# A graph network's prologue: degrees read one group later, x in fourteen buffers, its later groups loaded from ScalarE

## The chip, the cores and the metric

The kernel runs on one core of a Trainium2 chip. The metric is the device time of one execution in microseconds (us). One execution of the kernel before was also taken by the hardware profiler; its page and its trace are what the prediction reads.

## The reference

A graph of 12,500 nodes with 256 features and 200,000 edges, sorted by destination, goes through a three-layer graph convolution on the normalised features, with a residual, and then through a mixture of experts whose gates come from attention over a second edge list. What matters here is the start of the first part:

```python
deg_inv_sqrt = jnp.where(deg > 0, jax.lax.rsqrt(jnp.maximum(deg, 1.0)), 0.0)   # deg: edges into a node, and its own loop
norm = deg_inv_sqrt[src] * deg_inv_sqrt[dst]
h = x @ W
msg = h[src] * norm[:, None]
out = jax.ops.segment_sum(msg, dst, num_segments=n_nodes)   # + b; gelu after layers 1 and 2
...
x = x + _L0_gnn_ref(_layernorm(x, axis=-1), edge_index, ...)
```

So before the first layer can gather a row, every row of x must be normalised by its own mean and deviation and scaled by the square root of its node's degree, and the degrees have to be counted from the edge list.

## The kernel before

The nodes are cut into 98 tiles of 128 rows. The tiles go in 14 groups of seven (`groups`, `ROW_GROUP = 7`); the last tile is partly empty. Line numbers are those of the profile.

**The search.** `load_keys` reads sources and destinations, packs each edge into one key word, and `put_keys` writes the keys to DRAM (`keys_a`). If the edges had not been sorted, a branch (L611) would sort them; here it is jumped over. `starts` then finds each tile's first edge: it reads the first key of each of 128 rows (`a_first`, L426, issued from ScalarE), compares, gathers one whole row per tile (`a_row`, L438, an indirect transfer from GpSimd), and counts the keys below the tile's bound (L443). `mine` (L452) gathers each tile's keys, TensorE transposes them (L734), and VectorE makes from them the source numbers `a_src` and, as two small numbers `hi_p` and `lo_p`, each edge's place in its tile.

**x and the norms.** `xn` is one buffer for all 98 tiles. `load_x` fills it on SP's queue (L525, L528): `groups[:5]` before the branch in the program's text, the others after it; the scheduler has put two of those ahead of the branch as well. `norm(first, n)` takes mean and variance of `n` groups on VectorE (L589, L590) and the square root on ScalarE (L592). The calls are laid out by hand as filling between the steps of the search: groups 0 and 1, 2 and 3, 4 and 5, then 6 and 7 beside the degrees' way through DRAM, and 8 to 13 in the scaling loop.

**The count.** A loop over seven groups of 16 tiles (`TG16`, a grouping of its own) builds 24 one-hot pieces on VectorE (L782, L786; two buffers of each kind), multiplies them in 18 products on TensorE (L792) into a PSUM tile (`deg_ps`, two buffers), and reads the tile back on VectorE with a mask and a sum (L795, L797). `counts` is written to DRAM (L801) from SP and ScalarE, read back across partitions as `deg_t` (L804), and transposed; its inverse square root is `dis`.

**The scaling loop** (L1267 to L1288). For each group: three small VectorE instructions, then seven row tiles scaled and shifted, two on GpSimd, one on VectorE, four on ScalarE, and one write of the group to `tables[0]` on SP's queue (L1285). After all 14 groups, SP writes the same rows again, as `bases[0]`, each node's own share of the sum (L1288).

**The first layer.** `xn`'s room is then given back and used for the layers' tiles. A loop over overflow edges (`beyond`, no turns with these inputs) stands before the layer; its exit waits for what is under way. `cols_s` (L889) is GpSimd's first instruction after it, and then come the gathers from `tables[0]` (L1474), one per 128 edges, which go on through all three layers.

The order inside the stretches under `tc.manual_schedule()` is the order of the text; each engine runs its own instructions in order. SP and ScalarE both issue transfers; a transfer's issue waits until the one eight before it, over both, has landed.

Of the kernel before, what the change touches and what calls it, by code (L numbers as in the profile page):

```python
# [8 lines left out]
F32 = mybir.dt.float32  # L9
# [3 lines left out]
OP = mybir.AluOpType  # L13
AX = mybir.AxisListType
# [5 lines left out]
P = 128  # L20
D = 256
# [9 lines left out]
ROW_GROUP = 7  # L31
# [7 lines left out]
TG16 = 16  # L39
# [27 lines left out]
def gnn_ffn_kernel(  # L67
# [24 lines left out]
    nc = tc.nc  # L92
    N = x.shape[0]
    NT = (N + P - 1) // P
# [28 lines left out]
    groups = [(t, min(t + ROW_GROUP, NT)) for t in range(0, NT, ROW_GROUP)]  # L123
# [11 lines left out]
    CAP = caps[0] + (SPILL + P - 1) // P  # L135
# [381 lines left out]
        yield  # L517
        nc.vector.reciprocal(rstd, rstd)

    def load_x(t, g0, g1):  # L520
        if g1 * P > N:
            nc.vector.memset(t[:, : g1 - g0], 0.0)
        whole = min(g1, N // P)
        if whole > g0:
            nc.sync.dma_start(t[:, : whole - g0],  # L525
                              x[g0 * P : whole * P].rearrange("(t p) d -> p t d", p=P))
        if whole < g1:
            nc.sync.dma_start(t[: N - whole * P, whole - g0], x[whole * P : N])  # L528

    x2_d = dram.tile([NT * P, D], F32, name="x2_d")  # L530
    ht_d = dram.tile([M, ROW], F32, name="ht_d")
# [37 lines left out]
    bases = [dram.tile([NT, P, D], F32, name=f"base{i}") for i in range(3)]  # L569

    xn_cm = tc.tile_pool(name="xn", bufs=1)
    xn = xn_cm.__enter__().tile([P, NT, D], F32, name="xn")


    pre = ExitStack()
# [5 lines left out]
    rs = prep.tile([P, NT], F32, name="rs")  # L581
    sh = prep.tile([P, NT], F32, name="sh")
    SOONER = 5

    def norm(first, n):
        for g0, g1 in groups[first : first + n]:
            for t in range(g0, g1):
                six = prep.tile([P, 6], F32, name="six0", bufs=2)
                nc.vector.bn_stats(six, xn[:, t, :])  # L589
                nc.vector.bn_aggr(mv[:, t, :], six)  # L590
            nc.vector.tensor_scalar(rs[:, g0:g1], mv[:, g0:g1, 1], LN_EPS, None, op0=OP.add)
            nc.scalar.activation(rs[:, g0:g1], rs[:, g0:g1], AF.Sqrt)  # L592

    keys_cm = tc.tile_pool(name="keysA", bufs=1)
    with keys_cm as pool, tc.manual_schedule():
        key, n_falls = load_keys(pool, "a_", src, dst, EA, shifted=True)
        for g0, g1 in groups[:SOONER]:
            load_x(xn[:, g0:g1], g0, g1)
        none = pool.tile([P, tail_a], F32, name="none")
        nc.vector.memset(none, NO_EDGE)  # L600
        nc.scalar.dma_start(keys_a[EA:].rearrange("(p c) -> p c", p=P), none)
        put_keys(keys_a, key, EA)
        ps = lps.tile([P, P], F32, name="list_ps")
        for j in range(2):
            nc.tensor.matmul(ps[:1, :1], n_falls[:, j : j + 1], ones[:, 0:1], start=(j == 0),
                             stop=(j == 1))
        falls_i = prep.tile([1, 1], I32, name="falls_i")
        nc.vector.tensor_copy(falls_i, ps[:1, :1])
    unsorted = nc.values_load(falls_i[0:1, 0:1], min_val=0, max_val=EA,
                              skip_runtime_bounds_check_because="a count of edges")  # L610
    with tc.If(unsorted > 0):  # L611
        with tc.tile_pool(name="sortA", bufs=1) as pool, tc.tile_pool(
            name="sortA_ps", bufs=2, space=PSUM
# [20 lines left out]
    lpool = lists.enter_context(tc.tile_pool(name="lists", bufs=1))  # L634
    finding = starts(lpool, lps, "a_", keys_a, LA)
    next(finding)
    for g0, g1 in groups[SOONER:]:
        load_x(xn[:, g0:g1], g0, g1)
    norm(0, 2)
    next(finding)  # L640
    norm(2, 2)
    try:
        next(finding)
    except StopIteration as done:
# [1 line left out]
    nc.vector.tensor_copy(start_i, start_a)  # L646
    mine = lpool.tile([P, CAP * P + 1], F32, name="mine")
    read_keys(mine, keys_a, start_i[:, 0:1])
    norm(4, 2)


    spill = prep.tile([P, 12], F32, name="spill")
# [2 lines left out]
    ps = lps.tile([P, P], F32, name="list_ps")  # L655
# [12 lines left out]
    ps = lps.tile([P, P], F32, name="list_ps")  # L668
# [5 lines left out]
    ps = lps.tile([P, P], F32, name="list_ps")  # L674
# [13 lines left out]
    ps = lps.tile([P, P], F32, name="list_ps")  # L688
# [41 lines left out]
    for k0 in range(0, CAP, KG):  # L730
        n = min(KG, CAP - k0)
        ps = lps.tile([P, KG, NTP], F32, name="turn_ps")
# [18 lines left out]
    LO = 16  # L751
# [12 lines left out]
    with tc.tile_pool(name="deg", bufs=1) as pool, tc.tile_pool(  # L764
        name="deg_ps", bufs=2, space=PSUM
    ) as dps, tc.manual_schedule():
        same_i = pool.tile([P, 1], I32, name="same_i")
        nc.vector.tensor_scalar(same_i, pcol_i, TG16 - 1, None, op0=OP.bitwise_and)
        same_c = pool.tile([P, 1], F32, name="same_c")
        nc.vector.tensor_copy(same_c, same_i)  # L770
        same = pool.tile([P, TG16], F32, name="same")
        nc.vector.tensor_scalar(same, cols[:, :TG16], same_c, None, op0=OP.is_equal)
        counts = pool.tile([P, NTP // TG16, LO], F32, name="counts")
        NG = NTP // TG16
        step = 1
        for g0 in range(0, NG, step):
            n = min(step, NG - g0)
            w = slice(g0 * TG16, (g0 + n) * TG16)
            A = pool.tile([P, CAP, step, HI, TG16], BF16, name="hi_one", bufs=2)
            B = pool.tile([P, LO, CAP, step * TG16], BF16, name="lo_one", bufs=2)  # L780
            for v in range(HI):
                nc.vector.tensor_scalar(  # L782
                    A[:, :, :n, v, :], hi_p[:, :, w].rearrange("p k (g t) -> p k g t", t=TG16),
                    float(v), None, op0=OP.is_equal)
            for v in range(LO):
                nc.vector.tensor_scalar(B[:, v, :, : n * TG16], lo_p[:, :, w], float(v), None,  # L786
                                        op0=OP.is_equal)
            for g in range(n):
                s = slice(g * TG16, (g + 1) * TG16)
                ps = dps.tile([P, LO, TG16], F32, name="deg_ps")  # L790
                for k in range(CAP):
                    nc.tensor.matmul(ps, A[:, k, g].rearrange("p a t -> p (a t)"), B[:, :, k, s], start=(k == 0),  # L792
                                     stop=(k == CAP - 1))
                diag = pool.tile([P, LO, TG16], F32, name="diag", bufs=2)
                nc.vector.tensor_tensor(diag, ps, same[:, None, :].to_broadcast([P, LO, TG16]),  # L795
                                        op=OP.mult)
                nc.vector.tensor_reduce(counts[:, g0 + g, :], diag, axis=AX.X, op=OP.add)  # L797
        deg_v = deg_d.rearrange("(g t a b) -> a t g b", t=TG16, a=HI, b=LO)
        for a in range(HI):
            eng = nc.sync if a % 2 else nc.scalar  # L800
            eng.dma_start(deg_v[a], counts[a * TG16 : (a + 1) * TG16])  # L801
        norm(6, 2)
        deg_t = pool.tile([NTP, P], F32, name="deg_t")
        nc.scalar.dma_start(deg_t, deg_d.rearrange("(t p) -> t p", p=P))  # L804
        ps = lps.tile([P, P], F32, name="list_ps")
        nc.tensor.transpose(ps[:, :NTP], deg_t, ident[:NTP, :NTP])

        nc.vector.tensor_scalar(dis, ps[:, :NTP], 1.0, None, op0=OP.add)
# [456 lines left out]


    with tc.manual_schedule():  # L1267
        known = 8
        for i, (g0, g1) in enumerate(groups):
            if i + 1 >= known and i + 1 < len(groups):  # L1270
                norm(i + 1, 1)
            w = slice(g0, g1)
            nc.vector.reciprocal(rs[:, w], rs[:, w])
            nc.vector.tensor_tensor(rs[:, w], rs[:, w], dis[:, w], op=OP.mult)
            nc.vector.scalar_tensor_tensor(sh[:, w], mv[:, w, 0], -1.0, rs[:, w], op0=OP.mult,
                                           op1=OP.mult)
            for t in range(g0, g1):
                row, scale, shift = xn[:, t, :], rs[:, t : t + 1], sh[:, t : t + 1]
                if t % ROW_GROUP in (1, 4):
                    nc.gpsimd.tensor_scalar(row, row, scale, shift, op0=OP.mult, op1=OP.add)  # L1280
                elif t % ROW_GROUP == 6:
                    nc.vector.tensor_scalar(row, row, scale, shift, op0=OP.mult, op1=OP.add)
                else:
                    nc.scalar.activation(row, row, AF.Identity, bias=shift, scale=scale)
            nc.sync.dma_start(tables[0][g0 * P : g1 * P].rearrange("(t p) d -> p t d", p=P),  # L1285
                              xn[:, g0:g1, :])
        for g0, g1 in groups:
            nc.sync.dma_start(bases[0][g0:g1].rearrange("t p d -> p t d"), xn[:, g0:g1, :])  # L1288
    pre.close()
    xn_cm.__exit__(None, None, None)  # L1290

# [1 line left out]
    with tc.tile_pool(name="gwork", bufs=3) as work, tc.tile_pool(  # L1293
        name="gmsg", bufs=8
    ) as msg, tc.tile_pool(name="ghot", bufs=8) as hot, tc.tile_pool(name="later", bufs=1) as later, tc.tile_pool(
        name="sps", bufs=1, space=PSUM
    ) as sps, tc.tile_pool(name="gps_m", bufs=2, space=PSUM) as ps_m, tc.tile_pool(
        name="gps_d", bufs=3, space=PSUM
# [7 lines left out]
        for i, a in enumerate((att_src, att_dst)):  # L1306
# [4 lines left out]
                                    op=OP.mult)  # L1311
            nc.vector.tensor_reduce(wg[:, :, HE + i * HEADS : HE + (i + 1) * HEADS],
                                    wa.rearrange("p k (h e) -> p k h e", e=EXPERTS),
                                    axis=AX.X, op=OP.add)
# [114 lines left out]
        for layer in range(3):  # L1429
# [22 lines left out]
            with tc.manual_schedule():  # L1452
# [14 lines left out]
                for t in range(NT):  # L1467
                    pm = ps_m.tile([P, D + QUAD], F32, name="pm")
                    cap = caps2[t] if layer else caps[t]
                    for k in range(0, cap, QUAD):  # L1470
                        n = min(QUAD, cap - k)
# [9 lines left out]
                        else:  # L1481
# [3 lines left out]
                                         stop=False)  # L1485
                        for i in range(n):
                            nc.tensor.matmul(pm[:, :D], oh[:, i], m[:, i], start=False,  # L1487
                                             stop=False)
# [3 lines left out]
                        if k:  # L1492
                            i = k // QUAD - 1
# [16 lines left out]
                    for i in range(used):  # L1510
                        nc.tensor.matmul(pm[:, :D], oh[:, i], shared[:, i], start=False,  # L1511
                                         stop=(i == used - 1))
# [600 lines left out]
```

## Time and profile before

| What | Value |
|---|---|
| three timed runs, us | 7752.15, 7755.71, 7757.81 (median 7755.71) |
| the profiled execution, us | 7752.2, its span on the core 7750.4 |
| GpSimd busy | 5592.8 us (72%) |
| TensorE busy | 5482.8 us (71%) |
| VectorE busy | 4655.9 us (60%) |
| ScalarE busy | 990.6 us (13%) |
| start of the degree count (L782), us | 86.87 |
| counts begin to be written (L801), us | 145.18 |
| first table write (L1285), us | 165.08 |
| first gather of layer 0 (L1474), us | 247.21 |

The shares of busy time are averages over the whole execution; the first 247 us are a series of steps that wait for each other. Times in the trace count from the start of the span. A row of the timeline has start, duration, engine, line, instruction, what it writes from what, and in brackets how long the engine was idle before it and what ended that. `ACTq`, `SPq` and `POOLq` are the engines' sequencers, which issue transfers; the duration of such a row is that of the issue. A row of the waits has the instruction, what it waited for, the sum, the number of times and the longest.

### The profile page before, as it was taken

Reading aid. Unit: us, or ns where it says so; the run is one execution under the profiler, and the core shown is the slowest. Engines: PE = TensorE matmul, PEld = TensorE weight load, DVE = VectorE, ACT = ScalarE, POOL = GpSimd, SP = SyncE. Lnnn points to the kernel's source line nnn. Section 1 sums busy time; section 2 is a strip of 40 time slices with the busy share of each in tenths; the row PEclk is TensorE's granted clock in tenths of the full one; section 3 lists DMA queues with packets and bytes.
Section 4 is the critical chain, followed back from the end, with each engine's and each line's share of the span. In section 5 each row is a group of like instructions: output and inputs, shape, how many; then the busy total and the mean of one; then the engine's idle time right before and its main releaser. Section 6 shows DMA issues by size and latency. Waiting matters only on the chain. (4 is left out here: it accounts for less than half of the span.)

```text
span 7750.4 us, 76132 instructions
## 1 busy us (share of the span) xinstructions
PE 5482.8 (71%) x21346; PEld 4125.1 (53%) x21346; DVE 4655.9 (60%) x17434; ACT 990.6 (13%) x1890; POOL 5592.8 (72%) x5867
## 2 busy tenths in 40 slices
PE   1576767667767666666677776666666799889792
PEld 1455555556545555555555565555555566556561
DVE  6567776794427656665799985555555223334545
ACT  1012222000001111110100000000000122222221
POOL 0577777777767777777776777777777677777774
PEclk7788888888887888888898887887888899999896
DMA  4544444444444444444444444444444322222324
GB/s 152 168 126 126 123 125 124 123 123 125 126 117 124 124 126 125 126 126 127 132 125 117 130 135 132 133 132 133 132 134 132 105 69 68 60 47 45 106 45 132
DMA packets 535891, 906.71 MB, mean 117 GB/s; under 512 B 129568, under 2 KB 377470, under 8 KB 534878
## 3 DMA queue, kind: packets, MB, share of 16 engines
q0 software_dynamic: 260224, 620.67, 29.9%
q1 hardware_dynamic: 228182, 236.51, 9.4%
q10 hardware_dynamic: 47048, 44.46, 1.7%
q8 instruction: 182, 2.98, 0.2%
q14 instruction: 255, 2.09, 0.1%
HBM read 744.24 MB, written 156.95 MB: 116 GB/s over the span
## 5 line engine op out<-in xcount | busy, mean ns | idle before, releaser
L1474 POOL DMA_INDIRECT m<-table,u_src x2930 | 2805.0, 957 | 934.4 <-issue 802.3
L1487 PE MATMUL pm<-m,oh 128*128 128x256 f32 x8986 | 2840.1, 470 | 0.0
L1487 PEld LDWEIGHTS pm<-m,oh 128*128 128x128 f32 x8986 | 1988.4, 233 | 302.1 <-issue 0.6
L1474 POOL DMA_INDIRECT m<-table,a_src_l x1563 | 1488.8, 953 | 476.1 <-issue 414.9
L1484 PE MATMUL pm<-m,oh 128*128 128x4 f32 (+1 forms) x2346 | 453.4, 264 | 1698.6 <-DMA m<-table,u_src 539.6
L1484 PEld LDWEIGHTS pm<-m,oh 128*128 128x128 f32 x2346 | 408.0, 213 | 2072.6 <-issue 733.5
L1796 POOL DMA_INDIRECT g<-ht_d,b_src x1122 | 1074.7, 958 | 342.0 <-issue 334.0
L1448 DVE SCALAR_TENSOR_TENSOR oh<-psum_cols,u_lo,oh 128x128 f32<-128x128 f32 x2930 | 820.6, 338 | 0.0
L1593 PE MATMUL po<-w,hh 128*128 128x256 f32 x3136 | 704.5, 382 | 106.4 <-DVE x_now L1758 74.3
L1373 DVE TENSOR_TENSOR y<-pm,own 128x256 f32<-128x256 f32 x294 | 123.8, 421 | 1081.2 <-PE pm L1511 1049.7
L1593 PEld LDWEIGHTS po<-w,hh 128*128 128x128 f32 x3136 | 600.2, 192 | 229.9 <-DVE x_now L1758 76.7
L1585 PE MATMUL ps<-zt,w 128*128 128x512 f32 (+3 forms) x1728 | 695.3, 555 | 20.7 <-DMA zt<-zt_d 17.8
L1445 DVE TENSOR_SCALAR oh<-cols,u_lo 128x128 f32<-128x128 f32 x2930 | 667.7, 307 | 7.3 <-issue 4.4
L1324 ACT COPY z<-pd 128x256 f32<-128x256 f32 x392 | 145.8, 372 | 3570.9 <-PE pd L1319 3416.7
L1585 PEld LDWEIGHTS ps<-zt,w 128*128 128x128 f32 x1728 | 324.6, 191 | 335.9 <-issue 292.2
L1511 PE MATMUL pm<-shared,oh 128*128 128x256 f32 x1288 | 394.0, 439 | 29.6 <-DVE oh L1445 22.8
L1587 ACT ACTIVATE hh<-ps,b_c 128x512 f32<-128x512 f32 (+3 forms) x432 | 277.3, 647 | 955.9 <-PE ps L1585 954.7
L1330 PE MATMUL pd<-gw,z 128*128 128x256 f32 x1176 | 349.4, 426 | 2.4 <-ACT z L1324 2.4
L1445 DVE TENSOR_SCALAR oh<-cols,a_lo 128x128 f32<-128x128 f32 x1563 | 349.7, 303 | 0.0
L1756 DVE TENSOR_TENSOR y<-po,b_r 128x256 f32<-128x256 f32 x180 | 75.9, 423 | 427.9 <-PE po L1593 398.7
L1758 DVE SCALAR_TENSOR_TENSOR x_now<-po,gates,x_now 128x256 f32<-128x256 f32 x212 | 100.8, 481 | 376.6 <-PE po L1593 376.6
L1511 PEld LDWEIGHTS pm<-shared,oh 128*128 128x128 f32 x1288 | 282.7, 229 | 83.0 <-DVE oh L1445 26.3
(465 smaller groups left out, 5122.9 us busy)
## 6 DMA issues: line engine op xcount, KB each, us to landing
m<-table,u_src POOLq DMA_INDIRECT x2930
own<-base SPq DMA_DIRECT2D x294, 128.0 KB
table<-row SPq DMA_DIRECT2D x196, 128.0 KB
base<-row ACTq DMA_DIRECT2D x196, 128.0 KB
m<-table,a_src_l POOLq DMA_INDIRECT x1563
y_d<-y SPq DMA_DIRECT2D x40, 512.0 KB
y_all<-y_d SPq DMA_DIRECT2D x10, 2048.0 KB
g<-ht_d,b_src POOLq DMA_INDIRECT x1122
```

The costliest lines, as they stand in the source:

```text
L1324: nc.scalar.copy(z, pt)
L1330: nc.tensor.matmul(po[:, :width], z[:, k, :], w[:, k, :], start=(k == 0), stop=(k == 1))
L1445: nc.vector.tensor_scalar(oh[:, i], columns, first(i), None, op0=OP.is_equal)
L1448: nc.vector.scalar_tensor_tensor(oh[:, i], columns2, last(i), oh[:, i], op0=OP.is_equal, op1=OP.add)
L1474: nc.gpsimd.indirect_dma_start(out=m[:, i], out_offset=None, in_=tables[layer], in_offset=bass.IndirectOffsetOnAxis(ap=from_src[:, k + i, ...
L1484: nc.tensor.matmul(pm[:, D : D + n], oh[:, 0], m[:, :n, 0], start=(k == 0), stop=False)
L1487: nc.tensor.matmul(pm[:, :D], oh[:, i], m[:, i], start=False, stop=False)
L1511: nc.tensor.matmul(pm[:, :D], oh[:, i], shared[:, i], start=False, stop=(i == used - 1))
L1585: nc.tensor.matmul(ps[:, :n], w1[:, e, k, c * P : (c + 1) * P], zt[:, :n, k, :], start=(k == 0), stop=(k == 1))
L1587: nc.scalar.activation(hh[:, c, :n], ps[:, :n], AF.Gelu, bias=b1_c[:, e * FC + c : e * FC + c + 1])
L1593: nc.tensor.matmul(po, hh[:, c, i, :], w2[:, e, c, :], start=(c == 0), stop=(c == FC - 1))
L1796: nc.gpsimd.indirect_dma_start(out=g[:, c, :], out_offset=None, in_=ht_d, in_offset=bass.IndirectOffsetOnAxis(ap=b_src[:, c0 + c : c0 + c ...
```

## The change

Three things are changed. In the count, group g's PSUM tile is read by VectorE after group g+1's one-hot pieces have been built; group 4's norm is put before the last read. x has one buffer per group in place of one for all, and in the scaling loop SP writes the own rows of groups 0 to 5 each after the next group's table rows; those of 6 to 13 follow after the last table write. Groups 5 to 13 of x are loaded from ScalarE's queue after group 2's norm. The other norms move with it: group 3 after `mine`, 5 and 6 beside the degrees' way through DRAM, 7 to 13 in the scaling loop.

```diff
-    xn = xn_cm.__enter__().tile([P, NT, D], F32, name="xn")
+    xn_pool = xn_cm.__enter__()
+    xn = [xn_pool.tile([P, g1 - g0, D], F32, name=f"xn{i}") for i, (g0, g1) in enumerate(groups)]
...
     next(finding)
-    for g0, g1 in groups[SOONER:]:
-        load_x(xn[:, g0:g1], g0, g1)
     norm(0, 2)
     next(finding)
-    norm(2, 2)
+    norm(2, 1)
+
+    for g0, g1 in groups[SOONER:]:
+        load_x(xn[g0 // ROW_GROUP], g0, g1, nc.scalar)
...
     read_keys(mine, keys_a, start_i[:, 0:1])
-    norm(4, 2)
+    norm(3, 1)
...
+        def counted(g, ps):
+            diag = pool.tile([P, LO, TG16], F32, name="diag", bufs=2)
+            nc.vector.tensor_tensor(diag, ps, same[:, None, :].to_broadcast([P, LO, TG16]),
+                                    op=OP.mult)
+            nc.vector.tensor_reduce(counts[:, g, :], diag, axis=AX.X, op=OP.add)
...
+            ps = dps.tile([P, LO, TG16], F32, name="deg_ps")
+            for k in range(CAP):
+                nc.tensor.matmul(ps, A[:, k, 0].rearrange("p a t -> p (a t)"), B[:, :, k, :],
+                                 start=(k == 0), stop=(k == CAP - 1))
+
+            if g0:
+                counted(g0 - 1, held_ps)
+            held_ps = ps
+        norm(4, 1)
+        counted(NG - 1, held_ps)
...
-        norm(6, 2)
+        norm(5, 2)
...
-        known = 8
+        known = 7
+        SOON = 6
+
+        def put_own(i):
+            g0, g1 = groups[i]
+            nc.sync.dma_start(bases[0][g0:g1].rearrange("t p d -> p t d"), xn[i])
...
             nc.sync.dma_start(tables[0][g0 * P : g1 * P].rearrange("(t p) d -> p t d", p=P),
-                              xn[:, g0:g1, :])
-        for g0, g1 in groups:
-            nc.sync.dma_start(bases[0][g0:g1].rearrange("t p d -> p t d"), xn[:, g0:g1, :])
+                              xn[i])
+            if 1 <= i <= SOON:
+                put_own(i - 1)
+        for i in range(SOON, len(groups)):
+            put_own(i)
```

The matrix products, the one-hot pieces, the bytes loaded and the bytes written are the same as before; every instruction behind the scaling loop is the same.

More of the change, by code (lines that the diff above doesn't have):

```diff
@@ L518, in moments, with load_x @@
         nc.vector.reciprocal(rstd, rstd)
-    def load_x(t, g0, g1):
+    def load_x(t, g0, g1, eng=nc.sync):
         if g1 * P > N:
@@ L524, in load_x @@
         if whole > g0:
-            nc.sync.dma_start(t[:, : whole - g0],
+            eng.dma_start(t[:, : whole - g0],
                               x[g0 * P : whole * P].rearrange("(t p) d -> p t d", p=P))
         if whole < g1:
-            nc.sync.dma_start(t[: N - whole * P, whole - g0], x[whole * P : N])
+            eng.dma_start(t[: N - whole * P, whole - g0], x[whole * P : N])
     x2_d = dram.tile([NT * P, D], F32, name="x2_d")
@@ L588, in norm @@
                 six = prep.tile([P, 6], F32, name="six0", bufs=2)
-                nc.vector.bn_stats(six, xn[:, t, :])
+                nc.vector.bn_stats(six, xn[g0 // ROW_GROUP][:, t - g0, :])
                 nc.vector.bn_aggr(mv[:, t, :], six)
@@ L597, in gnn_ffn_kernel @@
         for g0, g1 in groups[:SOONER]:
-            load_x(xn[:, g0:g1], g0, g1)
+            load_x(xn[g0 // ROW_GROUP], g0, g1)
         none = pool.tile([P, tail_a], F32, name="none")
@@ L636, in gnn_ffn_kernel @@
     next(finding)
-    for g0, g1 in groups[SOONER:]:
-        load_x(xn[:, g0:g1], g0, g1)
     norm(0, 2)
     next(finding)
-    norm(2, 2)
+    norm(2, 1)
+    for g0, g1 in groups[SOONER:]:
+        load_x(xn[g0 // ROW_GROUP], g0, g1, nc.scalar)
     try:
@@ L787, in gnn_ffn_kernel @@
                                         op0=OP.is_equal)
[L788 to L797, printed above, removed]
+            ps = dps.tile([P, LO, TG16], F32, name="deg_ps")
[7 more added lines that the diff above has]
+        counted(NG - 1, held_ps)
         deg_v = deg_d.rearrange("(g t a b) -> a t g b", t=TG16, a=HI, b=LO)
@@ L1277, in gnn_ffn_kernel @@
             for t in range(g0, g1):
-                row, scale, shift = xn[:, t, :], rs[:, t : t + 1], sh[:, t : t + 1]
+                row, scale, shift = xn[i][:, t - g0, :], rs[:, t : t + 1], sh[:, t : t + 1]
                 if t % ROW_GROUP in (1, 4):
```

## The prediction

> **What bounds the kernel now.** I read the page's groups first. From about 247 us on, one queue sets the pace: GpSimd issues indirect gathers back to back.
>
> ```profile
> L1474 POOL DMA_INDIRECT m<-table,u_src x2930 | 2805.0, 957 | 934.4 <-issue 802.3
> L1474 POOL DMA_INDIRECT m<-table,a_src_l x1563 | 1488.8, 953 | 476.1 <-issue 414.9
> ```
>
> A gather takes 0.95 us, about 0.3 us of issue follows it, and nothing else ends its idle time. No gather is touched by the change, and in the order of the built programs every instruction behind the table writes is the same. So the change is worth what it moves the first gather, which stands at 247.21 us. (The page's chain shows only 0%; I use timelines.) Next I read VectorE's waits up to 250 us.
>
> ```profile
> DVE cols L1348 <- DMA base<-xn: 46.2, 1, 46.2
> DVE diag L795 <- PE deg_ps L792: 27.8, 7, 4.1
> DVE mv L590 <- DVEq L611: 10.1, 1, 10.1
> ...
> DVE a_junk L432 <- PE list_ps L429: 5.1, 1, 5.1
> ```
>
> Three stretches of the 247 us matter: counting (seven waits of 4 us), the search for each tile's first edge before it, and the write-out after it, whose last base row frees the first gather. One group of the count, in the timeline:
>
> ```profile
> 88.02 2.38 DVE L786 TENSOR_SCALAR lo_one<-lo_p 128x288 bf16<-128x288 bf16 x16
> ...
> 90.46 4.00 PE L792 MATMUL deg_ps<-lo_one,hi_one 128*128 128x256 bf16 x18 [12.99 <-DVE lo_one L786]
> ...
> 94.49 0.42 DVE L795 TENSOR_TENSOR diag<-deg_ps,same 128x256 f32<-128x256 f32 x1 [4.09 <-PE deg_ps L792]
> ```
>
> VectorE builds, TensorE multiplies, VectorE reads: never both at once. The search, in the timeline from 34 to 57 us:
>
> ```profile
> 34.67 0.33 ACTq L426 DMA_DIRECT2D a_first<-a_keys  x1
> ...
> 41.41 0.45 PE L429 MATMUL list_ps<-ident,a_first 128*128 128x128 f32 x1 [26.96 <-DMA xn<-in_x_dram]
> ...
> 43.60 1.13 POOL L438 DMA_INDIRECT a_row<-a_keys,a_r_i  x1 [42.06 <-DMA xn<-in_x_dram]
> ...
> 52.55 2.35 DVE L443 TENSOR_SCALAR_CACHE_REDUCE a_below<-a_row,bound 128x2048 bf16<-128x2048 f32 x1 [2.08 <-DMA a_row<-a_keys,a_r_i]
> ```
>
> A 512-byte read (a_first) takes 6.7 us from issue to use, while SP's x loads fill the queues. The transfer view of 0 to 72 us (slices of 1.8 us) shows them, and a sag from 27 to 36 us, as the key list is written amid the reads of x:
>
> ```profile
> GB/s 17 219 392 325 412 278 347 357 352 349 349 349 388 389 244 157 121 107 159 242 342 335 348 346 352 331 391 408 333 350 351 306 351 381 371 113 22 0 0 0
> ```
>
> Last the write-out, in the transfer view of 165 to 246.3 us (40 slices of 2.03 us):
>
> ```profile
> GB/s 171 335 336 335 335 335 348 342 338 338 348 336 346 337 347 118 347 33 281 319 339 335 354 337 339 339 350 338 339 334 352 335 338 339 349 340 340 347 347 136
> ```
>
> It is bandwidth: 25.7 MB at about 340, with one dip (118, 33, 281) near 195 to 203 us, when the tables issued so far were written and the next group was not yet scaled.
>
> **Part 1, counts read one group later: -23.4 us.** Now, from the first hi_one at 86.87 to the end of the last reduce at 145.05: 58.2 us. In the new order VectorE runs build 0, build 1, read 0, build 2, read 1 ... build 6, read 5, norm 4, read 6. A build is 3.53 us (86.87 to 90.40), a read 0.79 (94.49 to the next build at 95.28), a norm of one group 3.9 (144.97 to 148.88). Build 0 and 1 end at 93.93; read 0 waits for TensorE until 94.49; from then a group costs 3.53 + 0.79 = 4.32 on VectorE, more than TensorE's 4.00, so VectorE sets the pace: build 6 ends at 95.28 + 4 x 4.32 + 3.53 = 116.1, read 5 at 116.9, norm 4 at 120.8 (the last products end at 120.2, so it costs 0.6), read 6 at 121.6. That is 34.7 us for 58.2. A norm that today stands before the count is inside. Two buffers each for the operands and the products suffice: group g+2's products come after read g. Bounds: if TensorE needed 4.4 (18 times the 0.222 per product that 4.00 gives, and 0.4 of hand-over), -22.5; -24 if it runs faster and read 0 comes at once.
>
> **Part 2, later x loads and norms in another place: -12.3 us.** Groups 5 to 13 are loaded behind the table search, from ScalarE, after group 2's norm.
> - a_first: the same kind of small read on quiet queues, deg_t, took 1.84 us from issue (153.53) to TensorE (155.37), against 6.74 here: -4.9. Its issue also waited for the key list's writes, which shared the queues with x; VectorE came back from the jump (L611) at 33.67 with about 3 us of norm 1 left, so it can use the result from 36.8 on if the jump takes as long. Bounds 0 (reads of x still ahead of it) and -10 (jump and writes quicker too). I take -6, close to the row for deg_t.
> - a_row (1.05 MB): from a_r_i (42.63) to use at 52.55 it took 9.9 us. Alone: 1.0 to issue, 1.13, 1.84 for a quiet read, 3.1 at 340 GB/s: 7.1. Norm 2 (3.9) and the memset of group 13 (1.55, today at 1.42 us) fit before it. -2.8; bounds 0 and -4.4 (that work alone).
> - Norms ahead of the count: today 4 and 5 stand between start_i and the list (55.39 to 63.2); then only 3. -3.9, less a wait for `mine`, whose landing shows in no row; the first user that could wait starts at 67.68. I take -3.5; bounds 0 and -3.9.
> - ScalarE's ten issues queue ahead of group 3's Sqrt and of the cast to a_lo (81.31 today). SP's issues took up to some 3 us with the queues full (five in 17.31 us from 35.04), so ScalarE is busy until about 65 to 68; Sqrt 3 is needed only in the scaling and a_lo only at the first gather, so this costs nothing. Were the cover gone, it would be those 27 us at most.
> - Norms 5 and 6 replace 6 and 7 beside the degrees' round trip (deg_d to deg_t): 0. The weights' loads move ahead of the jump on SP, 1.2 MB while the queues are busy anyway: inside the bounds of a_first.
>
> **Part 3, a buffer per group and own rows amid the table's: -3.5 us.** The transfers are the same 28, with the same bytes. What changes is that own rows 0 to 4 are queued by the time group 6 is scaled, so the dip has work: (340-118) + (340-33) + (340-281), times 2.03 us, over 340 is 3.5 us. One more norm (3.9) in the scaling loop delays group 13 to about 207 us on today's axis, where 19 transfers of 2.7 us reach to 218: covered. The gathers do not start before the last own row is out, although each group has its own buffer: cols_s, the first instruction of GpSimd ahead of them, lies where group 13's buffer was (bytes 166,880 in 161,088 to 168,256), and the exit of the loop over overflow edges waits for all transfer semaphores. Bounds 0 and -5. [...]
>
> **Sum.** -23.4 - 12.3 - 3.5 = -39.2. The profiled execution took 7752.2 us (span 7750.4), which becomes 7713.0; the three timed runs have a median of 7755.7, which becomes 7716.5. I take 7715. About 0.2% (15.5 us) is what a measurement here tells from no change.
>
> **Rivals.**
> - A, chance 0.11: moving the loads only moves the collision. x now runs beside `mine` and the list, and the search gains nothing: 7755.7 - 23.4 - 3.5 = 7729. For it: x must cross the same queues at about 340 GB/s from whichever engine; against: a_first and a_row come before the first late load. [...] It is the moment, not the queue, that I count on.
> - B, 0.03: the gathers start once the tables are out, eight transfers of 2.7 us earlier: 7715 - 21 = 7694. Against: the two waits named.
> - C, 0.03: slower. Table and own rows alternate between two regions of HBM, and the write rate falls as it fell when key writes met x reads (107 to 159 GB/s, slices from 27 to 34 us). At 135 GB/s 25.7 MB take 190 us for today's 81: +109 - 35.7 = 7829. It decides once the stage is longer than 117 us, below 220 GB/s. Against: 340 GB/s while bases and tables already follow each other.
> - D, 0.03: the count does not overlap (VectorE and TensorE slow each other to today's 8.4 us): 7755.7 - 12.3 - 3.5 = 7740.
>
> **Numbers.** The forecast holds 0.80. The sum of the bounds is -22.5 to about -47 (not all ends together); with runs that differ by 3 us that is 7702 to 7732, which takes in rival A. Faster by over 0.2%: forecast, A and B, 0.94; D lies on the edge and goes to "within", 0.03; slower 0.03.
>
> **What would show it.** Seven groups of 4.3 us with no VectorE wait near 4 us but the first; a_first to TensorE in about 2 us and the next gather near 36; no dip in the write-out, which still ends with `base` freeing cols_s, some 39 us earlier, near 207. It is wrong if the period of the count stays over 5 us, if `mine` or a_row is waited for longer than today, or if a gather starts before the last own row.

## The result, and the profile after

| | before | after |
|---|---|---|
| median of six runs, us | 7758.2 | 7717.3 |
| profiled execution, us (its span) | 7752.2 (7750.4) | 7711.7 (7709.9) |
| first group of the count begins (hi_one), us | 86.87 | 75.53 |
| counts begin to be written, us | 145.18 | 110.02 |
| first table write, us | 165.08 | 129.53 |
| first gather of layer 0, us | 247.21 | 208.12 |

The ratio of the times is 0.9949, with a 95% interval of 0.9939 to 0.9960: 40.9 us between the medians, for a forecast of 40.7 between 7755.7 and 7715 (the prediction's own sum is 39.2). The first gather comes 39.09 us earlier, and the four rows of the table divide that: 11.34 in the search, 23.82 in the count, 0.39 in the degrees' way through DRAM, 3.54 in the write-out. The gathers themselves are as they were:

```profile
L1492 POOL DMA_INDIRECT m<-table,u_src x2930 | 2807.3, 958 | 934.0 <-issue 802.4
L1492 POOL DMA_INDIRECT m<-table,a_src_l x1563 | 1488.7, 952 | 476.1 <-issue 411.5
```

VectorE's waits up to 220 us (what waited, for what, the sum, the times, the longest):

```profile
DVE cols L1366 <- DMA base<-xn: 39.0, 1, 39.0
DVE mv L592 <- DVEq L613: 10.6, 1, 10.6
...
DVE a_junk L432 <- PE list_ps L429: 1.7, 1, 1.7
DVE a_below L443 <- DMA a_row<-a_keys,a_r_i: 1.0, 1, 1.0
...
DVE diag L781 <- PE deg_ps L800: 0.6, 1, 0.6
```

The seven waits for `deg_ps` are one, of 0.6 us. The wait at the branch (`DVEq L613`) has not shrunk. One group of the count, in the timeline:

```profile
87.39 0.41 DVE L781 TENSOR_TENSOR diag<-deg_ps,same 128x256 f32<-128x256 f32 x1
87.53 2.12 PE L800 MATMUL deg_ps<-lo_one,hi_one 128*128 128x256 bf16 x18 [2.22 <-DVE lo_one L796]
...
87.84 0.42 DVE L783 TENSOR_REDUCE counts<-diag 128x16 f32<-128x256 f32 x1
88.18 1.23 DVE L792 TENSOR_SCALAR hi_one<-hi_p 128x288 bf16<-128x288 bf16 x8
89.32 2.38 DVE L796 TENSOR_SCALAR lo_one<-lo_p 128x288 bf16<-128x288 bf16 x16
91.62 0.42 DVE L781 TENSOR_TENSOR diag<-deg_ps,same 128x256 f32<-128x256 f32 x1
```

VectorE goes from the read at once to the next build; its next read stands 4.23 us after this one, and TensorE works underneath. The search, in the timeline from 33 to 49 us:

```profile
33.74 0.33 ACTq L426 DMA_DIRECT2D a_first<-a_keys  x1
...
37.09 0.45 PE L429 MATMUL list_ps<-ident,a_first 128*128 128x128 f32 x1 [23.08 <-DMA wg<-in_L_ffn_W_gat_dram]
...
39.27 1.12 POOL L438 DMA_INDIRECT a_row<-a_keys,a_r_i  x1 [37.74 <-DVE six L591]
...
45.13 2.35 DVE L443 TENSOR_SCALAR_CACHE_REDUCE a_below<-a_row,bound 128x2048 bf16<-128x2048 f32 x1 [1.03 <-DMA a_row<-a_keys,a_r_i]
...
48.33 0.95 POOL L452 DMA_INDIRECT mine<-a_keys,start_i  x1 [7.93 <-DVE start_i L649]
```

a_first takes 3.35 us from issue to TensorE (6.74 before). The transfer view of 0 to 72 us (slices of 1.8 us) shows the queues at 5 to 101 GB/s from 27 to 41 us, where x was read before, and x mostly at 340 and more behind that:

```profile
GB/s 17 233 410 371 391 240 344 361 350 349 348 348 390 392 265 76 63 17 101 101 11 5 36 300 341 378 344 358 346 419 382 362 348 348 349 348 348 348 349 96
```

The write-out, in the transfer view of 129.5 to 207.5 us (slices of 1.95 us), has lost its dip, and the timeline behind it shows that its last `base` row still frees cols_s:

```profile
GB/s 170 335 336 339 339 340 335 348 335 353 337 337 338 347 341 337 340 347 340 336 343 342 337 339 348 338 339 337 348 338 336 349 337 336 339 348 338 347 349 69
```
```profile
207.45 0.30 POOL L899 IOTA cols_s<- 128x192 f32 x1 [37.94 <-DMA base<-xn]
...
208.12 1.00 POOL L1492 DMA_INDIRECT m<-table,a_src_l  x1 [0.38 <-issue]
```

### The profile page after: what moved, and what is told of

Its sections match the earlier page's. It is cut to its first block, busy times and chain, and to the rows that moved or that the text cites. A ratio compares the mean times of both kernels' runs of the same rounds, so it can differ in the third digit from the quotient of the medians.

```text
span 7709.9 us, 76137 instructions
## 1 busy us (share of the span) xinstructions
PE 5473.8 (71%) x21346; PEld 4119.8 (53%) x21346; DVE 4656.2 (60%) x17434; ACT 990.6 (13%) x1890; POOL 5593.8 (73%) x5867
## 5 line engine op out<-in xcount | busy, mean ns | idle before, releaser
L1492 POOL DMA_INDIRECT m<-table,u_src x2930 | 2807.3, 958 | 934.0 <-issue 802.4
L1492 POOL DMA_INDIRECT m<-table,a_src_l x1563 | 1488.7, 952 | 476.1 <-issue 411.5
L1529 PE MATMUL pm<-shared,oh 128*128 128x256 f32 x1288 | 392.3, 438 | 29.7 <-DVE oh L1463 22.5
```

What stands on the lines that cost most here:

```text
L1492: nc.gpsimd.indirect_dma_start(out=m[:, i], out_offset=None, in_=tables[layer], in_offset=bass.IndirectOffsetOnAxis(ap=from_src[:, k + i, ...
```

## The experiments

They ran on two other chips, e1 to e8 on one, e9 and e10 on the other. There the kernel before takes 9796 to 9808 us. In the changed kernel, run again as e9, the difference lies behind the first gather: 9543.9 us follow it in place of 7501.8, while the first gather itself stands at 207.84 for 208.12. A gather lasts as long there (956 ns); it is the idle time before the gathers that is longer (1535.5 and 774.2 us in e9 for the two groups shown above, in place of 934.0 and 476.1), and why is not known. So I judge by the first gather, in each run's own trace, against the 247.21 and 208.12 of the first chip, and give the ratio to the kernel before on the run's own chip with its interval. The search ends up to 1.2 us earlier or later from run to run, mostly by the wait at the branch.

| Kernel | first gather, us | ratio to before (95%) |
|---|---|---|
| e1 count alone | 219.55 | 0.9972 (0.9961 to 0.9982) |
| e2 counts read at once | 231.64 | 0.9986 (0.9977 to 0.9995) |
| e3 later x from SP | 214.83 | 0.9968 (0.9956 to 0.9980) |
| e4 the same, held | 208.55 | 0.9955 (0.9941 to 0.9968) |
| e5 own rows last | 215.06 | 0.9967 (0.9956 to 0.9979) |
| e6 one buffer | 208.48 | 0.9965 (0.9951 to 0.9978) |
| e7 own rows from the table | 178.45 | 0.9932 (0.9918 to 0.9945) |
| e8 weights later | 205.21 | 0.9960 (0.9947 to 0.9974) |
| e9 the changed kernel | 207.84 | 0.9958 (0.9944 to 0.9972) |
| e10 the best | 172.71 | 0.9916 (0.9902 to 0.9929) |

### e1: the count alone

The edit, on the kernel before: `counted` and the held PSUM tile, without a norm ahead of the last read.

```diff
+            if g0:
+                counted(g0 - 1, held_ps)
+            held_ps = ps
+        counted(NG - 1, held_ps)
```

> The kernel before with the late reading of the counts alone; x, norms and write-out as before, and no norm ahead of the last read. My theory: the parts add up, so the stretch from the first one-hot piece to the last sum goes from 58.2 us to 33 to 35 us (a period of 4.2 to 4.3 us, and the last read waits 2 to 4 us for the last products with no norm to cover it), and the time is 7758 - 24 = 7734 (7730 to 7738). Rival: the late reading needs the rest of the change (the norm ahead of the last read, or a TensorE that the other parts left with a higher clock): a period of 5 us or more, and 7742 or above.

Measured: first gather 27.7 us earlier than in the kernel before, 1.2 of it a search that ended earlier. The stretch is 31.9 us (85.63 to 117.54), shorter than I expected. The end of it, in the timeline:

```profile
114.50 2.13 PE L797 MATMUL deg_ps<-lo_one,hi_one 128*128 128x256 bf16 x18 [2.12 <-DVE lo_one L793]
...
116.66 0.42 DVE L778 TENSOR_TENSOR diag<-deg_ps,same 128x256 f32<-128x256 f32 x1 [1.43 <-PE deg_ps L797]
```

The last group's products take 2.13 us in place of 4.00, so the last read waits 1.4 us and not 2 to 4. The late reading does not need the rest of the change. It also shows what group 4's norm costs in the changed kernel: its stretch is 34.4 us, so 2.5 of the norm's 3.9 us are not hidden.

### e2: counts read at once

```diff
-            if g0:
-                counted(g0 - 1, held_ps)
-            held_ps = ps
-        norm(4, 1)
-        counted(NG - 1, held_ps)
+            if g0 == NG - 1:
+                norm(4, 1)
+            counted(g0, ps)
```

> The changed kernel with each group's counts read at once again; group 4's norm still ahead of the last read, all else as changed. My theory: the order makes the gain; VectorE again waits for each group's products, the products take 4.0 us again, the stretch is 58 us, and the time is 7717 + 23.8 = 7741 (7737 to 7744). Rival: much of the gain is the higher clock of TensorE in that stretch (0.90 in place of 0.68 in the two traces), which the rest of the change brought; then the products keep 2.1 to 3 us, a group costs about 3.5 + 0.1 + 2.1 + 0.8 = 6.5 us, the stretch is 46 us, and the time is about 7729.

Measured: first gather 231.64, 23.5 us after the changed kernel's, the stretch 58.3 us. From the waits and the timeline:

```profile
DVE diag L781 <- PE deg_ps L800: 24.0, 7, 4.1
```
```profile
94.89 3.84 PE L800 MATMUL deg_ps<-lo_one,hi_one 128*128 128x256 bf16 x18 [4.42 <-DVE lo_one L796]
```

The seven waits are back, and so are products of about 4 us, though all else is as changed. The faster TensorE came with the order and did not cause the gain; the rival falls. The changed kernel says the same: in its own timeline two groups have slow products and cost VectorE no wait:

```profile
95.99 2.96 PE L800 MATMUL deg_ps<-lo_one,hi_one 128*128 128x256 bf16 x18 [2.10 <-DVE lo_one L796]
100.22 3.93 PE L800 MATMUL deg_ps<-lo_one,hi_one 128*128 128x256 bf16 x18 [1.27 <-DVE lo_one L796]
```

### e3 and e4: the later loads from SP

e3 drops the queue from the call. e4 does so too and, behind `norm(2, 1)`, sets to zero one element of the first buffer, which holds the loads until the norm.

```diff
-        load_x(xn[g0 // ROW_GROUP], g0, g1, nc.scalar)
+        load_x(xn[g0 // ROW_GROUP], g0, g1)
```
```diff
+    nc.vector.memset(xn[SOONER][:, 0, 0:1], 0.0)
```

> The changed kernel with the later x loads issued by SP, at the same place of the text. SP has nothing of group 2's norm to wait for, so in its order they stand where they stood before: two ahead of the branch, the others right behind it. My theory: ScalarE matters only because its Sqrt of group 2 stands ahead of them and holds them until 42 us; without that a_first takes 6 to 7 us to TensorE again and a_row 9 to 10, and the time is 7717 + 7.4 = 7724 (7721 to 7728). Rival: the front's gain came from the norm taken out of it and from nothing else, or from ScalarE's queue taking less of the queues' share: 7717 and 7 us still gained in the first case; no change of a_first in either.

> The changed kernel with the later x loads on SP, and one element of the first of their buffers set to zero by VectorE after group 2's norm, so that they start at the same moment, some 42 us, as from ScalarE. My theory: the moment counts and the queue does not: 7717, 7713 to 7721, a_first 3.3 us and a_row 6.8 us as in the changed kernel. Rival: the queue counts (SP's transfers get in the way of the small reads wherever they stand, or ScalarE's ten issues hold something up that SP's do not): 7724 or more in the first case, below 7712 in the second.

Measured: e3 gives 214.83, 6.7 us later than the changed kernel (7.4 expected). The timeline shows x ahead of the search again, and a_first at 6.29 us; a_row's use comes 9.9 us after a_r_i:

```profile
32.85 18.03 SPq L525 DMA_DIRECT2D xn<-in_x_dram  x6
33.71 0.34 ACTq L426 DMA_DIRECT2D a_first<-a_keys  x1
...
40.00 0.45 PE L429 MATMUL list_ps<-ident,a_first 128*128 128x128 f32 x1 [25.36 <-DMA xn<-in_x_dram]
```

e4 gives 208.55, with x issued at 42.36 us, a_first at 3.05 us and a_row at 6.7. So ScalarE's queue is only the means: its Sqrt of group 2 stands ahead of the loads. Issued by SP at the same moment, they give 208.55 us for 208.12.

### e5 and e6: own rows last, and one buffer

```diff
-            if 1 <= i <= SOON:
-                put_own(i - 1)
-        for i in range(SOON, len(groups)):
+        for i in range(len(groups)):
             put_own(i)
```
```diff
+    xn_all = xn_pool.tile([P, NT, D], F32, name="xn")
+    xn = [xn_all[:, g0:g1] for g0, g1 in groups]
```

The first cut is e5, the second e6; both are on the changed kernel.

> The changed kernel with all fourteen own-row writes after the last table write; the buffers stay separate. My theory: the place of the writes makes the gain of the write-out. Groups 7 to 13 are scaled one in 4.87 us and a group's table rows take 2.7 us, so the tables catch up with the scaling near group 12 and the queues stand idle for 3 to 4 us before group 13; the first gather moves from 208.1 to 211.5 to 212.5 us, and the time is 3.5 to 4 us longer than the changed kernel's. Rival: the separate buffers make it (the order of the writes is indifferent): first gather at 208.

> The changed kernel with x in one buffer again, of which the fourteen groups are slices; order of loads, norms and writes as changed. My theory: the separate buffers change nothing by themselves, each instruction waits for the rows that it touches: first gather at 208 (207.5 to 209), time as the changed kernel's. Rival: with one buffer the scaling of a group waits for the own rows of the group before, which are still being written: group 13's table would come several us later and the first gather at 211 or later.

Measured: e6 gives 208.48, the changed kernel's within the scatter of the search: the separate buffers do nothing by themselves. e5 gives 215.06; from its first table write to the first gather it takes 85.8 us, against 78.6 as changed and 82.1 before. The place of the own rows is worth 7.2 us, twice what I expected. The transfer view of 129.5 to 212 us (slices of 2.06 us) says why:

```profile
GB/s 229 335 336 337 336 335 339 348 338 349 335 347 221 271 50 348 52 272 173 145 335 334 340 337 339 341 348 340 338 340 336 350 338 339 337 348 340 339 349 348
```

SP's issues in the timeline name the place: groups 9, 10, 11 and 12 are issued alone at 154.35, 159.25, 164.09 and 168.97 us, one in 4.9 us, the pace of the scaling. The tables catch up with it at group 9 and not at 12. What the seven low slices between the 13th and the 20th (221 to 145) fall short of 340 comes to 7.3 us.

### e7: own rows from the table

```diff
-            nc.sync.dma_start(own, bases[layer][t])
+            nc.sync.dma_start(own, bases[layer][t] if layer else tables[0][t * P : (t + 1) * P])
```

and no `put_own` at all.

> The changed kernel without the own-row writes of the first layer: each tile's own rows are read from the table, which holds the same numbers. The sum over overflow edges, which has no turns with these inputs, would add to rows that are no longer read. My theory: the 12.8 MB of own rows hold the first gather for as long as they are written after the last table group; without them the stage ends when group 13's table rows have landed, issued at 169.4 us, so the first gather is at 172 to 176 us in place of 208.1, and the time is 32 to 36 us shorter than the changed kernel's. Rival: the own rows' reads, in the same table as the gathers, slow the first layer, and part of that comes back: first gather the same, but the rest of the execution 5 us or more longer. A second rival: it is not the writes but the exit of the loop over overflow edges that costs time: first gather no earlier than 185.

Measured: 178.45, 29.7 us earlier, or 31 with the search that was 1.2 late. From the timeline and the waits:

```profile
130.50 42.05 SPq L1301 DMA_DIRECT2D table<-xn  x14
```
```profile
DVE cols L1362 <- DMA table<-xn: 8.3, 1, 8.3
```

The last table group is issued at 172.2 us, landed some 5 us later, and frees cols_s. My 172 to 176 is missed even with the 1.2 us taken off: I had allowed too little for that landing, and the 169.4 us was misread. In the changed kernel that is the twelfth table write, the last one in a view that ends at 172 us; two more are issued behind it, up to 177.2 us. The exit of the loop adds nothing that shows (the first gather is at 178.45, not at 185 or later), and the first layer does not give the gain back: the span behind the first gather is 9557.3 us, against 9554.4 to 9561.9 in the seven other runs on this chip. The ratio is 0.0023 to 0.0033 below those of e4 and e6, whose first gathers are the changed kernel's and which ran on this chip too: 22 to 32 us.

### e8: the weights later

```diff
+    for w in (*(w[:, 0, 0:1] for w in Ws), *(b[:, 0:1] for b in bs), wg[:, 0, 0:1]):
+        nc.vector.memset(w, 0.0)
```

after `norm(2, 1)`.

> The changed kernel with the loads of the first part's weights held back until group 2's norm (one element of each is set to zero by VectorE there, seven instructions), so that between 20 and 42 us the queues hold the key list's writes and the small reads alone. My theory: the weights share the queues with a_first; with them away it takes 1.8 to 2.4 us to TensorE in place of 3.35, VectorE's wait at the branch stays at 10 us, and the first gather comes 1 us earlier, 206.5 to 207.7. Rival: the wait at the branch is itself for the full queues; then it shrinks by 3 us or more, and the first gather comes at 204 or earlier.

Measured: 205.21, 2.9 us earlier. Waits and timeline:

```profile
DVE mv L592 <- DVEq L613: 6.7, 1, 6.7
...
DVE spill_i L715 <- DMA mine<-a_keys,start_i: 1.4, 1, 1.4
```
```profile
30.52 0.34 ACTq L426 DMA_DIRECT2D a_first<-a_keys  x1
...
32.80 0.45 PE L429 MATMUL list_ps<-ident,a_first 128*128 128x128 f32 x1 [18.17 <-DVE rs L1290]
```

Both theories hold in part. a_first takes 2.28 us (2.13 in e10), against 2.7 to 3.6 in the seven traces with the weights ahead of it, so the weights were in its way; and the wait at the branch falls from 10.6 to 6.7 us, which I had denied. In ten other traces, with x or the weights in the queues, it is 9.5 to 11.3 us; with the queues left alone, here and in e10, 6.7 and 7.6. Of the 4.4 us by which `mine` is issued earlier, 1.5 are lost again: from its issue to its use it takes 10.3 us in place of 8.8, with the weights now in the queues beside it as well as x. Why the wait at the branch is shorter with the queues left alone, no view shows.

### e9 and e10: the changed kernel again, and a better one

e10 holds the weights as e8 does and drops the own-row writes as e7 does, with the overflow kept: table and base are halves of one tensor, the loop over overflow edges copies the one to the other on its first turn, and a register says which half is read. Group 7's norm stands between the square root and the reciprocal of `dis`.

```diff
+    both = dram.tile([2 * NT, P, D], F32, name="both")
...
+    nc.vector.tensor_scalar(own_at, n_ov, 0.0, float(NT), op0=OP.is_gt, op1=OP.mult)
+    own_reg = nc.values_load(own_at[0:1, 0:1], engines=[mybir.EngineType.SP], ...)
...
+                with tc.If(i < 1):
+                    nc.sync.dma_start(bases[0], both[0:NT])
...
+            nc.sync.dma_start(own, bases[layer][t] if layer else
+                              both[bass.ds(own_reg + t, 1)].rearrange("o p d -> (o p) d"))
...
+        norm(7, 1)
```

> The changed kernel once more, beside the same runs of the kernel before as the next one. My theory: everything up to the first gather is as in its own trace: first gather at 207.5 to 209 us, 39 to 40 us earlier than before. Rival: the 39 us are those of one chip, and the stretches come out otherwise here: first gather outside that range.

> The changed kernel with three things more: the own rows of the first layer are read from the table (and from a copy of it with the overflow edges added, if there are any: a register chooses); the weights' loads are held until group 2's norm; and group 7's norm stands ahead of the scaling loop, beside the degrees' way through DRAM. My theory: the gains add, since they lie in three stretches one after the other: 30 us from the own rows (with the 1.2 us that the search was late in that run taken off), 2.9 from the weights, 2.3 to 2.7 from the norm (3.9 less some 1.2 that it stands in the way of the degrees): first gather at 171 to 174 us, and 75 us less than the kernel before, 36 less than the changed one. Rival: the reads at a register's address cost SP so much that tiles finish late and the first layer takes longer: first gather the same, the time 10 us or more above that.

Measured: e9's first gather at 207.84, its ratio to before 0.9958. e10's at 172.71, its ratio 0.9916 (0.9902 to 0.9929): 82 us of 9800 (70 to 96), of which the 74.5 us by which the first gather is earlier than before are seen in the trace: 39.4 by e9 and 35.1 more, for 34 to 37 expected. That compares one trace of each; what group 7's norm gives was not run by itself. Timeline of e10:

```profile
128.19 38.33 SPq L1314 DMA_DIRECT2D both<-xn  x14
171.97 0.30 POOL L912 IOTA cols_s<- 128x192 f32 x1 [7.53 <-DMA both<-xn]
...
172.71 1.13 POOL L1502 DMA_INDIRECT m<-both,a_src_l  x1 [0.44 <-issue]
```

The span behind the first gather is 9540 us, and 9544 in e9, one trace each: the reads at a register's address cost nothing that shows. The copy for overflow edges has no turn with these inputs, so that path has not been measured.

## Why the prediction was right, point by point

The three mechanisms are those forecast. That the sum (39.2) meets the 39.09 us of the first gather so closely is partly luck: the parts miss by 0.4 and 1.0 us in opposite directions, and the degrees' way through DRAM, put at 0, gave 0.39. The last 1.5 us from 7716.5 to the 7715 taken have no reason in the prediction; they lie within the scatter of the runs.

- **Part 1 (-23.4 forecast, -23.8 measured).** Right, and e1 and e2 show that the order does it (26.3 us alone, 23.5 when undone). The 0.4 us are the period, 4.23 us for 4.32; the first read waited 0.64 us, about as worked out (0.56), and no other read waited. One remark in it was wrong without harm to the sum: group 4's norm does not cost 0.6 us against a stretch without it but 2.5, since products of 2.1 us, not 4.0, leave it little to hide behind. The stretch is VectorE's work end to end, with the norm in it.
- **Part 2 (-12.3 forecast, -11.3 measured).** a_first is the mis-sized term: a_r_i ends 4.3 us earlier, for 6. I took the row of deg_t (1.84 us), and it is 3.35, because the weights (1.2 MB), which I had set "inside the bounds", were in the same queues; without them, in e8, a_first takes 1.1 us less and the wait at the branch is 3.9 us shorter. The signs named for this part missed with it: the next gather is issued at 39.27 and not near 36 (the -6 itself would have put it at 37.6). a_row gave 3.1 (forecast 2.8), the norm 3.9 (3.5); `mine` is waited for by TensorE alone, 0.65 us, which the kernel before did not have: one of the signs named for a wrong forecast came true, and cost nothing, since VectorE had work of its own until then. ScalarE's issues end at 65.8 us, as reckoned, and delay nothing.
- **Part 3 (-3.5 forecast, -3.5 measured).** Right in sum and incomplete in its parts. I read the gain from the dip of the kernel before, 3.5 us, and called the extra norm in the scaling loop covered (its 19 transfers of 2.7 us reach to 216.4 and not 218, still past the 207). It is covered only because the own rows now stand between: without them it makes the stage 3.7 us longer (85.8 for 82.1), and the own rows take back 7.2. Full slices stay at 335 to 353 GB/s.
- **Rival A** (the search gains nothing, 7729) fell: 7.4 us of the front are a_first and a_row, and e3 loses 6.7. The moment counts, not the queue, as e4 shows.
- **Rival B** (gathers start once the tables are out) fell for the reason given; e7 puts the price of that wait at some 30 us, where eight transfers had given 21. The rest is that the tables too are out earlier, no longer sharing the bandwidth with six groups of own rows (their issue ends at 172.6 us in place of 177.2).
- **Rival C** (own rows between table rows slow the writes) fell: the stage runs at 340. Its precedent was misread, as was the sag in the transfer view on which it rests. In the kernel before, from 22 to 27 us, ScalarE's queue moves 1.05 MB of keys and SP's 0.63 MB of x, together at a mean of 340 GB/s; from 27 to 36 us, where the slices are slow, ScalarE's moves 0.01 MB, and VectorE waits at the branch until 33.67. What slows the reads of x there stays open.
- **Rival D** (no overlap) fell: 4.23 us a group.

## What to carry to other kernels

Read a PSUM tile one step later whenever the trace shows VectorE building, TensorE multiplying and VectorE reading in turn: the gain here was about the product's length a step (4.00 us; a group went from 8.4 to 4.23), and the steps that remain tell which engine bounds it. When a bulk load is moved away from a small read, look at what else then lies in the queues beside it (here the weights, 1.1 of a_first's 3.35 us), and at branches, whose wait was longer here whenever there was traffic (9.5 to 11.3 us against 6.7 and 7.6). Ask of each write whether the same bytes are already somewhere: the write that ended the stage here was a second copy.

## What the runs showed of the hardware

The same 126 products of the count took 27.2 us of TensorE before and 19.5 after. One window row of each, around the count (last three columns: granted clock, DMA share, GB/s):

```profile
86.90:145.00 58.10, 27.20 (x126) 17.77 (x126) 30.02 (x184) 0.00 (x0) 0.00 (x0) 0.68 0.00 1
```
```profile
75.50:110.00 34.50, 19.46 (x126) 14.61 (x126) 33.35 (x199) 0.21 (x1) 0.00 (x0) 0.90 0.00 1
```

Over the whole count the granted clock is 0.68 where TensorE pauses 4.4 us between groups, and 0.90 where it pauses 2.2 us or less. (Both rows count the clock as full up to the end of the first 18 products, although these take some 4 us; behind them the kernel before has 0.63.) e2, with 4.42 us again, is back at products of 3.5 to 4.0 us. On these means the longer pause goes with the lower clock. The two slow groups of the changed kernel, shown at e2, do not fit that: their 18 products take 2.96 and 3.93 us at clocks of 0.69 and 0.53, after pauses of only 2.10 and 1.27 us. e1 and e9 have such a pair too (2.73 and 4.00, 3.26 and 3.77 us). What lowers the clock there stays open. On the mean, the overlap made the hidden engine faster as well, and here that shortened the cover for a norm.
